# Decoder of two layers on one Trainium2 core: TensorE's order pinned by a fixed table in the stage of the heads of 16 and layer 0's experts

## The chip, the cores and the metric

One core of one Trainium2 chip runs the whole decoder in one launch. The metric is the device time of one execution in microseconds (us); several executions are compared by their median. The core has five engines that work at the same time, each through a queue of its own: TensorE (PE in the profile, with PEld for its loads of the stationary operand), VectorE (DVE), ScalarE (ACT), GpSimd (POOL) and SyncE (SP, which here issues DMAs). They meet at semaphores: an instruction waits until the results that it needs, or the buffer that it writes, are free.

## The reference

Everything is in 32-bit floats; the batch has 8 rows of 256 tokens of width 256. Cut to what matters here:

```python
x = x + L0_attn(layernorm(x))          # 16 heads of 16, rotary, biases
x = x + L0_xattn(ctx, layernorm(x))    # 16 heads of 16, keys and values are ctx itself, masked by length
x = x + L0_ffn(layernorm(x))           # experts that choose tokens, below
x = x + L1_attn(layernorm(x))          # 16 heads of 16, rotary, causal
x = x + L1_xattn(layernorm(x), ctx)    # 16 heads of 64, one null key and value
x = x + L1_ffn(layernorm(x))           # 8 experts, top 1, and a shared one

def L0_ffn(x):
    t = log(clip(x @ gate_w, 1e-6))                    # [b, n, 8]
    for _ in range(8):                                 # Sinkhorn
        t = t - logsumexp(t, axis=tokens)
        t = t - logsumexp(t, axis=experts)
    vals, idx = top_k(exp(t) per expert, n // 8)       # each expert takes 32 tokens of a row
    out = (x[idx] @ experts[e]) * vals
    return zeros.at[idx].set(out)                      # the last writer of a token wins
```

The case is about the first four lines (and of the fifth only the tables that are made for it).

## The kernel before, in words

x stays in SBUF as 16 tiles of 128 tokens by 256; tiles 2b and 2b+1 are row b of the batch. The first stage is a list of 24 *units*, each the attention of one row. Units 0 to 15 are layer 0's, in groups of four: self-attention of rows b and b+1, then cross-attention of the same two. Units 16 to 23 are layer 1's causal self-attentions. Beside them run the experts of layer 0, `chosen_experts`, for two rows at a time, as soon as the cross-attentions of those rows are done; layer 1's unit of a row needs the experts of the row.

A unit's **core** (`attention`, line 309) has four steps (c, kt): half c of the heads, half kt of the keys. A step is `scores` (eight matmuls of heads of 16, packed 32 rows a piece, into one tile `st`, line 326), two exponentials on ScalarE of 128x1024 each (`pT`, line 337; in layer 1 GpSimd then clears what is not causal, line 340), and `values` (sixteen matmuls into `o`, line 362, where the padded values carry a column of ones that yields the denominator). After kt = 1, `divided_T` (lines 395 to 405) on VectorE turns `o` by query, divides, and turns it back: `by_q`, `dens`, `att`, `attT`.

Ahead of a self-attention's core, `prepare` makes the layernorm (`norm_stats`, lines 252 to 257: statistics and small sums on VectorE, the power on GpSimd, then `normed`, line 261), transposes it (`tr`, line 284, copied by ScalarE), projects queries and keys (`qk`) and values (`v`) through `product` (line 275) for each half t of the tokens, turns them by rotary (lines 410 to 426), adds them up (`qkr`, line 462, on GpSimd for t = 0 and VectorE for t = 1), transposes keys and queries (`kT`, `qps`, line 471), and makes the masked queries `qm` (lines 305 on VectorE and 306 on ScalarE). Behind the core, `end` projects the output (`ao`) and adds it to x (line 489). A cross-attention needs only the transposed norm (`qpsx`, line 540) ahead, and `oR` (line 554) behind.

The experts: for each of two rows a norm (`xnb`), its transpose, the gate's product `lg` and `g` (line 641); then eight times a column sum by TensorE (`cs`) and a chain of six instructions on VectorE (lines 650 to 657); then `vps` (line 663), the top tokens of each expert (lines 669 to 673, a chain of twenty-one instructions on VectorE), which go through DRAM (`slots`, lines 676 to 682) and come back as rows and columns (`idx_row`, `by_half`, `cps` at line 687); then for each row `pick` (line 699, GpSimd), the rows taken by TensorE (`rps`, `rT`), the experts' products `y`, and the products that put them back (`back`, added at line 755).

[...] `mm`, three buffers of one bank, for all products and transposes; `scp`, one buffer of four banks, for `st`; `op`, one buffer of one bank, for `o`. So scores wait until the exponentials of the step before have read `st`, and values of a new half wait until `by_q` has read `o`.

**The order before.** `core()`, `prepare()`, `end()` and `chosen_experts()` are generators. The loop over units (below) advances the core and hands out pieces of the neighbours (`beside`) and of the experts at each yield; this is the program's order. From it a planner makes every engine's queue by its own estimate of when operands are ready, and by priorities: the last three quarters of the scores are drawn forward by `tc.high_priority(offset=AHEAD)`, with `AHEAD = 400` instructions. So the planner may put scores, or one of the other products, between the matmuls of a group of values. Six empty yields stand between the DMAs of the slots and `cps`. `tables_x` (norms, `wn`, `nvs`, `nvw` of the next stage) comes before the last unit's core, `weights_x` when all experts are done.

## Time and profile before

| what | value |
|---|---|
| time before, median of 3 runs | 1284.95 us (1284.14 to 1289.21) |
| the profiled execution, its own time | 1284.25 us |
| its span in the trace | 1282.4 us |
| first stage, first scores to the last of its products | 25.5 to 541 us |
| median of a scores matmul (128x512), of a values matmul | 587 ns, 379 ns |
| exponential of 128x1024, with and without the bias of the keys | 1110 ns, 1019 ns |
| `by_q` transpose on VectorE | 716 ns |
| power of a norm on GpSimd | 699 ns |

The profile is of one execution. Its page gives each engine's busy time and share of the span, then the span in 40 slices, each digit the busy share in tenths; PEclk is the TensorE clock that was granted, in tenths of full speed. Every group of instructions is named by line, engine, operation and the tiles that it writes and reads. "idle before" is time in which an engine stood still ahead of a group, with the instruction that released it. A timeline row has start, duration, engine, line, and the number of instructions; matmuls of 32-bit floats appear twice in these counts. Matmuls are pipelined, so the distance from start to start of two groups tells more than a duration. A row of stretches has the stretch, its length, then busy time and number of instructions of PE, PEld, DVE, ACT and POOL, the mean granted clock, the DMA share and GB/s.

### The profile page before, as it was taken

To read this page: it belongs to the slowest core of one execution; us is meant where nothing else is said; L and a number is where in the kernel's file an instruction comes from. 1 tells how busy PE (TensorE), PEld (TensorE's weight loads), DVE (VectorE), ACT (ScalarE), POOL (GpSimd) and SP (SyncE) were. 2 spreads that over 40 slices of the span, in tenths; PEclk is the share of its full clock that TensorE was granted. 3 is DMA by queue.
4 is the path that set the end of the run, shared out by engine and by line. 5 is a ranking of instruction groups with operands and counts; after the bars stand their busy time and mean duration, and the time that the engine had idled before them with its cause. 6 is when DMAs were issued, how large, how long until landed. Compare 5 with 4: busy or idle time off the path is not lost.

```text
span 1282.4 us, 28726 instructions
## 1 busy us (share of the span) xinstructions
PE 1200.1 (94%) x12188; PEld 726.8 (57%) x12188; DVE 585.2 (46%) x1632; ACT 438.6 (34%) x672; POOL 372.0 (29%) x450
## 2 busy tenths in 40 slices
PE   6889899799898989799999999999999999999997
PEld 2324344344344444457666666667676466888874
DVE  5455665755675765532333233324232657222213
ACT  2445445444434434213223232323142332122220
POOL 4322132141143454203242332414142514200004
PEclk8999899799899999999999999999999999999999
DMA  9990000000000041001010101020211205499934
GB/s 300 341 296 18 9 26 9 18 18 1 9 1 2 10 149 75 1 17 35 18 35 18 35 18 35 18 51 2 51 29 33 76 1 214 181 409 403 407 132 135
DMA packets 46923, 116.59 MB, mean 91 GB/s; under 512 B 8272, under 2 KB 30400, under 8 KB 42432
## 3 DMA queue, kind: packets, MB, share of 16 engines
q1 hardware_dynamic: 38912, 92.74, 21.2%
q0 software_dynamic: 5152, 18.89, 4.0%
q10 hardware_dynamic: 2720, 3.02, 0.7%
q8 instruction: 98, 1.61, 0.5%
q14 instruction: 41, 0.34, 0.1%
HBM read 104.00 MB, written 27.93 MB: 103 GB/s over the span
## 4 chain that ended last, share of the span: by engine, by line
PE 74%; DVE 9%; POOL 2%; issue 2%; ACT 1%; DMA 1%; SPq 0%; POOLq 0%; ACTq 0%; DVEq 0%
PE h L275 7%; PE v L275 7%; PE k L275 6%; PE o L362 5%; PE wo L275 5%; PE ox L1387 4%; PE stx L1348 4%; PE out L1765 3%; PE out L1582 3%; PE h L970 3%; PE st L326 3%; PE q L275 3%; PE qk L275 2%; PE tr L284 2%; PE fm L275 2%
## 5 line engine op out<-in xcount | busy, mean ns | idle before, releaser
L337 ACT ACTIVATE pT<-st 128x1024 f32<-128x1024 f32 (+1 forms) x128 | 110.6, 915 | 103.2 <-PE st L326 93.1
L362 PE MATMUL o<-pT,padv 128*32 128x256 f32 (+1 forms) x1536 | 127.0, 384 | 11.7 <-DVE by_q L395 4.0
L1354 POOL TENSOR_TENSOR both<-pTx 128x512 f32<-128x512 f32 x64 | 82.1, 1308 | 44.6 <-ACT pTx L1352 38.9
L362 PEld LDWEIGHTS o<-pT,padv 128*32 128x32 f32 x1536 | 49.7, 112 | 75.6 <-issue 46.8
L275 PE MATMUL h<-xrT,w 128*64 128x128 f32 (+1 forms) x1936 | 87.0, 250 | 1.3 <-issue 1.3
L337 ACT ACTIVATE pT<-st,kbias 128x1024 f32<-128x1024 f32 x64 | 67.8, 1110 | 57.5 <-PE st L326 57.4
L275 PEld LDWEIGHTS h<-xrT,w 128*64 128x64 f32 x1936 | 84.5, 137 | 4.0 <-issue 1.8
L1352 ACT ACTIVATE pTx<-stx 128x1024 f32<-128x1024 f32 x64 | 62.3, 1021 | 41.5 <-PE stx L1348 26.2
L963 DVE TENSOR_TENSOR midr<-sl,h 128x128 f32<-128x128 f32 x102 | 29.4, 288 | 101.7 <-PE h L275 68.4
L275 PE MATMUL qk<-l_wqkv,xnT 128*64 128x512 f32 x256 | 72.0, 630 | 1.8 <-DVE col L689 1.1
L326 PE MATMUL st<-qm,kT 32*128 32x512 f32 (+1 forms) x512 | 67.1, 594 | 3.0 <-ACT qm L306 1.5
L962 ACT ACTIVATE sl<-h 128x128 f32<-128x128 f32 (+1 forms) x114 | 35.3, 310 | 95.6 <-PE h L275 56.6
L1348 PE MATMUL stx<-qTx,kTx 64*128 64x256 f32 x512 | 64.3, 391 | 2.5 <-ACT pTx L1352 2.5
L340 POOL TENSOR_SCALAR_AFFINE_SELECT pT<-pT 128x512 f32<-128x512 f32 x64 | 41.7, 662 | 79.6 <-ACT pT L337 79.6
L1387 PE MATMUL ox<-pTx,vx 128*64 128x256 f32 x512 | 62.3, 385 | 0.0
L257 POOL TENSOR_TENSOR lnrs<-lnve,mhalf 128x2 f32<-128x2 f32 x48 | 33.8, 708 | 97.0 <-DVE lnve L255 76.1
L275 PE MATMUL wo<-wout_x,oT 128*64 128x256 f32 x512 | 58.0, 379 | 0.0
L1348 PEld LDWEIGHTS stx<-qTx,kTx 64*128 64x128 f32 x512 | 46.1, 186 | 20.3 <-ACT pTx L1352 7.6
L395 DVE STREAM_TRANSPOSE by_q<-o 128x512 f32<-128x512 f32 x48 | 34.2, 713 | 48.6 <-PE o L362 48.3
L1442 POOL TENSOR_TENSOR oT<-oT,rs 128x512 f32<-128x512 f32 x30 | 37.3, 1274 | 65.6 <-DMA rs<-rd 65.6
L257 POOL TENSOR_TENSOR lxrs<-lxve,mhalf 128x2 f32<-128x2 f32 x8 | 5.6, 702 | 155.4 <-DVE sc L1101 123.9
L1387 PEld LDWEIGHTS ox<-pTx,vx 128*64 128x64 f32 x512 | 33.9, 136 | 26.4 <-issue 12.1
(366 smaller groups left out, 2182.6 us busy)
## 6 DMA issues: line engine op xcount, KB each, us to landing
w<-packs SPq DMA_DIRECT2D x22, 1408.0 KB
w<-packs SPq DMA_DIRECT2D x22, 768.0 KB
rs<-rd SPq DMA_DIRECT2D x16, 512.0 KB
packs<-L_ffn_w_eDF SPq DMA_DIRECT2D x8, 704.0 KB
packs<-L_ffn_w_eDF SPq DMA_DIRECT2D x8, 640.0 KB
packs<-L_ffn_w_eFD SPq DMA_DIRECT2D x8, 640.0 KB
ctxT<-ctx_T SPq DMA_DIRECT2D x8, 512.0 KB
wkv_x<-L_xattn_Wkv POOLq DMA_DIRECT2D x1, 4096.0 KB, 15.6
```

The lines of the kernel that those rows point to most:

```text
L257: nc.gpsimd.tensor_tensor(rs[:, :n], ve[:, :n], mhalf[:, :n], ALU.pow)
L275: nc.tensor.matmul(out[h], lhsT[:, h], rhs, start=start, stop=stop, skip_group_check=True)
L326: nc.tensor.matmul(st[:, r, :, :n], kT[rows, c, bass.ts(kt, P)], qm[rows, c, :, q0:], start=True, stop=True,)
L337: nc.scalar.activation(pT[:, :, :, :n], st[:, 2 * k : 2 * k + 2, :, :n], AF.Exp, scale=scale, **kb)
L340: nc.gpsimd.affine_select(out=pT[:, :, :, :P], in_=pT[:, :, :, :P], compare_op=ALU.is_ge, fill=0.0, base=0, pattern=[[0, 2], [0, 2], [1, P ...
L362: made = nc.tensor.matmul(o[HP * j : HP * j + HP, m, q0:], v_pad[:, kt, 8 * c + 2 * j + m, :], pTs[j // 2][:, j % 2, m, : S - q0], start=k ...
L970: nc.tensor.matmul(h, shared["ws13"][:, c, lo : lo + P], shared["xnT"][:, c, bass.ts(q, 2 * S)], start=c == 0, stop=c == 1)
L1348: nc.tensor.matmul(st[:, g, kt, :], kT[rows, c, bass.ts(kt, P)], qT[rows, c, :], start=True, stop=True)
L1352: nc.scalar.activation(pT, st, AF.Exp, scale=scale)
L1354: nc.gpsimd.tensor_tensor(both, pT[:, :, 0, :], pT[:, :, 1, :], ALU.add)
L1387: nc.tensor.matmul(o[XD * g : XD * (g + 1), i, :], v[:, kt, 2 * (c2 + i) + g, :], pT[:, g, kt, :], start=kt == 0, stop=kt == 1, skip_group ...
L1582: nc.tensor.matmul(ps, mid[:, i, lo : lo + P], w2[:, i, :], start=i == 0, stop=i == NFC - 1)
```

## The change

The arithmetic is the same, and so is the number of matmuls. What changes is who decides TensorE's order. The generators `core`, `prepare` and `end` become methods: a class `Core` with `scores(step)` and `values(step)`, and on the attentions `norm`, `rows`, `heads(t)`, `vals(t)`, `begin` and `out`. The program runs within `tc.manual_schedule(engines={PE})`, so that TensorE's queue is in program order, while the planner still orders the other engines' queues. For every step (n, k) of unit n the program is: the scores of the next step (at k = 3 those of the next unit's first step), the values of this step, then everything that a fixed table `sides[n, k]` holds. The table is filled once: norm of unit n at (n-2, 2), rows at (n-2, 3), heads at (n-1, 0), values at (n-1, 1), `begin` (kT, qps, qm) at (n-1, 2), output at (n+1, 0), in layer 1 at (n+1, 2) and (n+1, 3), and pieces of the experts by counts. `AHEAD` goes; instead `SOON = 60` raises the priority of norms, of `divided_T` and of the chain behind each column sum. In the experts the norm of the first row becomes a piece of its own, the norm of the second stands behind the first one's `lg`, the six empty yields become one, and `pick` is made one row ahead. `tables_x` moves behind the last unit's steps (after the last values, before the last output), `weights_x` to the end of unit 20, `slot_tables` to (3, 3), and `add_up` to (0, 1).

By lines, after: product 276, transposes 285, scores 328, exponentials 339, values 365, `divided_T` 390 to 400, `qkr` 460, output add 485, `qpsx` 539, `oR` 549, `g` 640, the chain 652 to 659, the top chain 671 to 675, `cps` 688, `pick` 699.

```diff
-AHEAD = 400
+SOON = 60
...
-    def attention(kT, qm, v_pad, scale, causal, bias, dens):
+    class Core:
+        def scores(self, step):
...
             for r in range(4):
-                with tc.high_priority(offset=AHEAD if r else 0):
-                    nc.tensor.matmul(
+                nc.tensor.matmul(
...
-        ahead = scores(0)
-        yield
-        for step in range(4):
-            now = ahead
-            if step % 2 == 0:
-                o, begun = op.tile([P, 2, S], F32, tag="o", name="o"), {}
-            if step + 1 < 4:
-                ahead = scores(step + 1)
-                yield
-            values(step, now, o, begun)
-            if step % 2:
-                divided_T(attT[:, step // 2, :], o, dens[:, step // 2, :])
-            yield attT
+        def values(self, step):
+            c, kt, q0 = self.queries(step)
+            if kt == 0:
+                self.o, self.begun = op.tile([P, 2, S], F32, tag="o", name="o"), {}
...
+            if kt:
+                with tc.high_priority(offset=SOON):
+                    divided_T(self.attT[:, c, :], o, self.dens[:, c, :])
...
+        def norm(self):
+            with tc.high_priority(offset=SOON):
+                self.xn = work.tile([P, 2, D], F32, tag="xn", name="xn")
+                mv, rs = norm_stats([x[:, 2 * self.b + t, :] for t in range(2)], 1e-5, small, "ln")
+                for t in range(2):
+                    self.head = normed(self.xn[:, t, :], x[:, 2 * self.b + t, :], mv, rs, t)
+
+        def rows(self):
+            self.xnT = transposed(self.xn, work, mm, "xnT")
+            self.qkr = work.tile([P, 2, 2 * D], F32, tag="qkr", name="qkr")
...
+        def normed_rows(b):
+            with tc.high_priority(offset=SOON):
+                mv, rs = norm_stats([x[:, 2 * (b0 + b) + t, :] for t in range(2)], 1e-5, small, "ln")
+                for t in range(2):
+                    normed(xn[:, 2 * b + t, :], x[:, 2 * (b0 + b) + t, :], mv, rs, t)
+
+        normed_rows(0)
+        yield
         for b in range(nb):
-            mv, rs = norm_stats([x[:, 2 * (b0 + b) + t, :] for t in range(2)], 1e-5, small, "ln")
-            for t in range(2):
-                normed(xn[:, 2 * b + t, :], x[:, 2 * (b0 + b) + t, :], mv, rs, t)
             xnT = transposed(xn[:, 2 * b : 2 * b + 2, :], work, mm, "xnT")
             yield
...
+            if b + 1 < nb:
+                normed_rows(b + 1)
             yield
...
-        for _ in range(6):
-            yield
+        yield
         cps = mm.tile([P, 2, 2 * nb], F32, tag="mm", name="cps")
...
-        for b in range(nb):
+        def picked(b):
             pick = bwork.tile([P, 2, S], F32, tag="pick", name="pick")
-            put = bwork.tile([P, 2, S], F32, tag="put", name="put")
             for t in range(2):
                 nc.gpsimd.tensor_scalar(pick[:, t, :], idx_row[:, b, :], tokid[:, t : t + 1], None, ALU.is_equal)
-            yield
+            picks.append(pick)
+
+        picked(0)
+        yield
+        for b in range(nb):
...
+    for n, u in enumerate(units):
+        if u.__class__ is SelfAttention:
+            beside(n - 2, 2, u.norm)
+            beside(n - 1, 0, partial(u.heads, 0), partial(u.heads, 1))
+            beside(n - 1, 1, partial(u.vals, 0), partial(u.vals, 1))
+            beside(n - 1, 2, u.begin)
+            beside(n - 2, 3, u.rows)
+            if u.layer:
+                beside(n + 1, 2, partial(u.out, 0)) if n + 1 < len(units) else None
+                beside(n + 1, 3, partial(u.out, 1)) if n + 1 < len(units) else None
+            else:
+                beside(n + 1, 0, partial(u.out, 0), partial(u.out, 1))
+    for n, u in enumerate(units):
+        if u.__class__ is CrossAttention:
+            beside(n - 1, 0, u.norm)
+            beside(n - 1, 1, u.vals)
+            beside(n - 1, 2, u.begin)
+            beside(n + 1, 0 if n == 15 else 2, u.out)
+    beside(0, 1, add_up)
+    beside(3, 3, slot_tables)
+    for i in range(3):
+        n = 4 * i + 5
+        experts_at(i, n, 2, 2, 1, 1)
+        experts_at(i, n + 1, *((1, 2, 2, 2) if i == 2 else (1, 1, 1, 1)))
+        experts_at(i, n + 2, *((0, 1, 0, 0) if i == 2 else (0, 1, 1, 1)))
+        if i < 2:
+            experts_at(i, n + 3, 1, 0, 0, 1)
+            experts_at(i, n + 4, 0, 1, 1, 1)
+            experts_at(i, n + 5, 0, 1, 1, 1)
+        else:
+            experts_at(i, n + 3, 1, 1, 1, 1)
+            experts_at(i, n + 4, 0, 1, 1, 1)
+    experts_at(3, 16, 1, 1, 1, 1)
+    experts_at(3, 17, 1, 2, 2, 2)
+    experts_at(3, 18, 1, 1, 1, 0)
+    experts_at(3, 19, 0, 1, 1, 2)
+    experts_at(3, 20, 1, 2, 0, 0)
...
+    order.enter_context(tc.manual_schedule(engines={mybir.EngineType.PE}))
...
     for n, u in enumerate(units):
...
+        for k in range(4):
+            if k < 3:
+                u.core.scores(k + 1)
+            elif n + 1 < len(units):
+                units[n + 1].core.scores(0)
+            u.core.values(k)
+            for made in sides[n, k]:
+                made()
...
+    wn, nvw, hot8 = tables_x(wd, wq_x, wout_x, nkrow, nvcol)
+    order.close()
+    for t in range(2):
+        units[-1].out(t)
```

## The prediction

> **What bounds the kernel now.** I read the page first, then the busy time by stage, then TensorE's waits in the first stage, then its timeline. On the page TensorE is the busy engine:

> ```profile
> PE 1200.1 (94%) x12188; PEld 726.8 (57%) x12188; DVE 585.2 (46%) x1632; ACT 438.6 (34%) x672; POOL 372.0 (29%) x450
> PEclk8999899799899999999999999999999999999999
> ```

> The 9s of PEclk give way to 8s and a 7 in the first third: there TensorE partly runs at half clock. The orders of all five engines behind the stage of the heads of 16 (from the context's first product on, 541 us) are the same in both kernels, so only 25 to 541 us counts:

> ```profile
> 25.00:123.00 98.00, 86.43 (x664) 32.91 (x668) 46.02 (x116) 48.84 (x58) 26.02 (x34) 0.94 0.72 240
> 123.00:213.00 90.00, 81.87 (x764) 37.35 (x759) 56.56 (x179) 41.20 (x49) 24.15 (x28) 0.92 0.06 16
> 213.00:303.00 90.00, 81.51 (x764) 37.31 (x756) 56.57 (x179) 41.31 (x49) 24.15 (x28) 0.92 0.06 16
> 303.00:368.00 65.00, 57.29 (x546) 26.04 (x542) 42.10 (x150) 30.59 (x35) 11.99 (x15) 0.92 0.02 5
> 368.00:541.00 173.00, 152.36 (x1528) 76.71 (x1524) 107.95 (x306) 69.31 (x105) 71.35 (x99) 0.99 0.12 44
> ```

> PE (third figure) is busy for 82 of 90 us; DVE (the next but one) has 33 us free in each such stretch. So DVE isn't the bound by its sum, only by the order in which it does things. TensorE's waits in this stage, about 54 us in all, lie behind DVE results (total, times, longest):

> ```profile
> PE cs L275 <- DVE g L657: 15.6, 13, 2.9
> PE tr L284 <- DVE qkr L462: 7.6, 9, 2.7
> PE oR L554 <- DVE attT L405: 7.5, 8, 1.5
> PE o L362 <- DVE by_q L395: 4.0, 3, 2.8
> ```

> The longest, then what follows it, and a group of values cut in two:

> ```profile
> 149.92 0.62 PE L275 MATMUL cs<-g,ones 128*64 128x16 f32 x8 [2.92 <-DVE g L657]
> ...
> 152.00:156.00 4.00, 3.54 (x30) 1.15 (x26) 2.55 (x9) 2.81 (x3) 1.61 (x2) 0.50 0.00 0
> 156.00:160.00 4.00, 3.08 (x18) 0.80 (x12) 2.43 (x9) 0.36 (x1) 0.00 (x0) 0.50 0.00 0
> ...
> 143.20 0.62 PE L362 MATMUL o<-pT,padv 128*32 128x256 f32 x2
> 143.75 1.14 PE L326 MATMUL st<-qm,memk 32*128 32x512 f32 x8
> ```

> After 2.92 us idle the granted clock (the third figure from the end) is 0.50 until about 163. The two rows of o take 0.55 us to the next start, though a sixteenth of a whole group (1.0 us, start to start) would be 0.06 each.

> [...] here 2.76 us (at 75) was enough, and 2.75 (at 476) wasn't, and the way back took up to 14 us. [...]

> **The change, part by part.** No matmul is added or removed. TensorE's order becomes next scores, values, side products, and the side products wait in that order.

> (1) TensorE's work in the stage, from start-to-start times of uncut groups: scores, 80 x 1.07 + 16 x 0.65 = 96; values, 80 x 1.0 + 16 x 0.57 = 89; fifteen self-attentions' qk (2 x 1.83), v (2 x 0.96), three groups of transposes (0.5 each) and ao (1.9), 9.0 each, 135, and 2 of unit 0; eight cross attentions at 1.3, 10; four expert pairs at 16.7 (two tr 1.0, two lg 1.14, eight cs 2.8, vps and cps 0.8, two of rps, y and back 11.0), 67; tables 6. Sum 405. Before took 515.5 (25.5 to 541): 405, 54 idle, about 23 of clock (54 us ran at half rate, by slices of 4 us, of which some 23 are loss), and 33 left, of which the cut groups (120 pieces of o rather than 96, 34 groups cut, 0.5 each) are 17. I take the whole 33 as gone. So 110 us are to be had, and the question is what waits come.

> (2) Gate of the exponentials. One st buffer: two exponentials of 1.02 and the latencies make it 3.27 us from scores to scores (3.45 in cross). A step with 1.07 + 1.0 of its own and under 1.2 of side products waits: 12 us in units 0 to 4 (about 1.0 a step), 6 in units 5 to 12. Where the masked queries follow transposes in the same slot the next scores can start 1.70 us after the transposes (513.73/514.26 to 515.96), with 1.0 of values over it only if these stand behind; in layer 1 four such starts and steps give 11. Sum 29.

> (3) Group starts: the experts' transposes (tr of xnb) stand right behind ao in units 5, 9 and 13. On DVE six statistics (0.4 each), six aggregations (0.12 to 0.18), two ao adds (0.42) and three small adds come first, then three powers one after another on POOL (L257, 0.70 each, of which the first two count), then xnx, then xnb: 4.3 + 1.0 + 1.6 + 1.1 = 8.0 us from ao's start; ao itself is 1.95. 6.0 us of stall, three times: 18. Scores, values and everything else queue behind it. In before the same transpose at 305.11 had no wait.

> (4) by_q (L390 after) behind LN on DVE, with one o buffer: the next values wait. In unit 6 DVE's queue has 26 instructions between ao's add and by_q: adds 0.8, six statistics 2.4, six aggregations 0.8, one chain of the column sums 0.9, small adds 0.4, four norms 1.5, 6.9 in all, and 1.6 of waiting for two powers; from 1.0 after ao's start by_q comes 9.5 to 10 later, where the values of step 2 are due 5.8 after it: 4.3. The same count gives unit 2 2.8, unit 10 2.5, and unit 14 7.0 (two column sums and LN together). Sum 17.

> (5) The top chain (DVE, 5.4 us in before, 159.45 to 164.85) stands ahead of by_q and of qm in units 8 and 12: o waits 1.7, scores for qm 2.3, cps for the slots' DMA 1.4, 5.4 each; the same in unit 15 4.5, in units 18 and 19 3.2. Sum 18.5. In before six idle steps lay over the slots (vps to pick 11.4 us, 158.4 to 169.8); now two steps of some 5 us do, which is where the 1.4 comes from. Pick stands one batch further ahead on POOL, before the powers and the causal masks: 0 to 1 us, taken at 0.

> (6) Two cs in one slot wait for DVE's chain of six (1.5 us with its latencies, up to 1.9): units 14 and 17, 3.6 + 7.3 = 11.

> (7) The end: nvw now stands after the last values, with byk and its sums on DVE before it; no attention lies beside it. 5 us (before: 1.6).

> (8) On SP's and POOL's queues: the slot tables three steps later, the weights of the next stage (4096 KB on POOL's queue, 15.6 us to landing) behind step (20,3), three units of some 17 us before their use: nothing. add_up in (0,1) lies beside scores; its ps no longer waits 2.0 for bvw ahead of the first units, and I let the first scores start at 24.5 rather than 25.5.

> Waits 29 + 18 + 17 + 18.5 + 11 + 5 = 98.5. Clock: stalls of over 2.75 us at three group starts cost 7 each as at 149.92 (14 us at half rate), with 6 for the others: 27. Stage end: 24.5 + 405 + 98.5 + 27 = 555, against 541: +14. The profiled run's own time is 1284.25 (span 1282.4 and 1.85 about it), 0.7 below the median; 1284.25 + 14 = **1298**.

> Bounds of what no row of before shows. Group starts: 3 us each if DVE's adds and statistics run closer than I walk them, 7 with every semaphore late: 9 to 21. Clock: 10 [...] to 60 (eight stalls at 7). The 33 left over: half may belong to the switches between products and stay: 0 to +16.

> **Rivals.** (A) Not slower: DVE keeps up. DVE has 33 us of slack in 90, and with LN, sums and divisions raised in priority, its chains may begin as soon as data is there. Items 3 to 6 are 64.5 us; at half, 32 go, and the clock falls to 12 (no stall over 2.75): 24.5 + 405 + 66 + 12 = 507.5, or 1284.25 − 33.5 = 1251. It decides as soon as waits and clock together stay under 111.5 (I have 125.5). For it: the whole pipeline has 110 us to win. Against: before's own 4.0 us of o behind by_q, at one buffer, shows DVE's queue already being late.
> (B) The pinned order is worth the planner's: waits 88, clock 23, 541 as before: 1284.
> (C) The clock compounds: eight stalls at 7 us rather than 27 in sum, 1298 + 29 = 1327. For: 54 us ran cold in before with hardly any idle over 2.7. [...]
> That the order isn't what the change says is out: TensorE's queue holds 96 whole groups of values in place of 120 pieces.

> **How the numbers follow.** Likeliest 0.48 (own range 1287 to 1312); A 0.26 (1235 to 1278); B 0.12; C 0.14. About 0.5% (6.4 us) is what a measurement tells from no change. Faster takes A less its edge, 0.25; same B and a little of the two beside it, 0.14; slower 0.61. The range reaches into A and C: 1258 to 1324.

> **What would show it.** Right: tr waiting for xnb three times for about 6 us, o for by_q in units 6, 10 and 14, PEclk 5 or 6 after each, stretch 123 to 303 longer than 180 us. Wrong: no wait of tr on xnb above 3 us, or a st-to-st of about 3.3 through units 0 to 4 with a stage end below 530; then A.

## The result

The changed kernel takes 1294.03 us (median of 5 runs, 1291.79 to 1296.44), the kernel before 1285.04 beside it (1284.14 to 1289.21): a ratio of 1.0063, 95% interval 1.0041 to 1.0085. It is a little slower, by 9 us.

The page of the changed kernel, TensorE's busy row and its granted clock:

```profile
PE 1171.2 (91%) x12188; PEld 721.7 (56%) x12188; DVE 582.7 (45%) x1632; ACT 438.2 (34%) x672; POOL 374.4 (29%) x450
PEclk8999998998998999899999999999999999999999
```

TensorE is busy for 29 us less with the same instructions, and yet the span is 9.9 longer: the work got cheaper, the waits grew. The stretches of the changed kernel cover the same units as those shown of before (0 to 4, 5 to 8, 9 to 12, 13 to 15, 16 to the end of the stage; stretch, length, busy time of PE, PEld, DVE, ACT and POOL, granted clock):

```profile
25.00:114.50 89.50, 72.88 (x650) 29.58 (x650) 42.08 (x102) 48.48 (x57) 23.75 (x30) 0.94 0.79 262
114.50:192.60 78.10, 62.51 (x630) 28.79 (x630) 47.05 (x159) 40.13 (x47) 16.45 (x20) 0.93 0.05 15
192.60:275.80 83.20, 71.96 (x759) 34.66 (x759) 53.64 (x178) 41.30 (x49) 24.34 (x28) 0.96 0.06 17
275.80:351.00 75.20, 57.70 (x612) 28.46 (x612) 46.95 (x162) 30.93 (x36) 14.38 (x18) 0.92 0.02 5
351.00:548.40 197.40, 166.27 (x1609) 83.00 (x1609) 116.98 (x331) 69.61 (x106) 79.04 (x107) 0.93 0.11 40
```

Before, these were 98, 90, 90, 65 and 173 us. So the change wins 27 us up to unit 12, gives 10 back in units 13 to 15, and 24 more from unit 16 on. The stage ends at 548.4, where it ended at 541.4, 7.0 later. The other 2.9 us of the span lie behind the stage and aren't the change's: that part has the same orders in both, the two traces agree in it within 0.1 us for its first 578 us, and over all kernels of this document it takes 739.6 to 746.1 us.

TensorE's waits in the stage, changed kernel (total, times, longest):

```profile
PE st L328 <- ACT qm L307: 29.1, 19, 5.3
PE tr L285 <- DVE xnb L262: 14.6, 3, 4.9
PE st L328 <- ACT pT L339: 14.3, 17, 2.1
PE cs L276 <- DVE g L659: 11.6, 5, 4.5
PE o L365 <- DVE by_q L390: 7.3, 5, 1.9
PE o L365 <- POOL pT L344: 5.6, 4, 2.5
PE nvw L829 <- DVE nvs L825: 4.3, 1, 4.3
```

Two of the kernel before:

```profile
PE st L326 <- ACT qm L306: 1.5, 3, 0.7
PE st L326 <- ACT pT L337: 1.3, 2, 1.1
```

The largest growth is in the scores, which wait for the masked queries and for the exponentials: 43.4 us, where it was 2.8. The transposes of xnb follow with 14.6.

To compare kernels I split the stage, from its first scores to the next stage's first product, into three: TensorE's idle time (the waits' view, which also counts about 1 us ahead of the first scores), what the lowered clock cost (one minus the granted clock), and the rest, which is work at full clock with all switches between products. Beside it stands the number of unbroken groups in TensorE's queue: matmuls of one line and the same tiles that follow each other.

| kernel | stage end | idle | clock | rest | groups |
|---|---|---|---|---|---|
| before | 541.4 | 56.4 | 26.3 | 433.3 | 477 |
| changed | 548.4 | 92.8 | 34.1 | 396.1 | 386 |

With the order in whole groups the work is 37 us cheaper; 36 were paid in waits and 8 in clock. The clock term of one profile is one draw: worked out from span and mean granted clock, the loss over the whole program is 38.3 us on average over the five executions of the changed kernel, and the executions of the kernel before spread by 3.4 to 3.8 us (standard deviation).

### The profile page after: what moved, and what is told of

The parts are those of the page before. It is cut to its first block, busy times and chain, and to the rows that moved or that the text cites. A ratio compares the mean times of both kernels' runs of the same rounds, so it can differ in the third digit from the quotient of the medians.

```text
span 1292.3 us, 28714 instructions
## 1 busy us (share of the span) xinstructions
PE 1171.2 (91%) x12188; PEld 721.7 (56%) x12188; DVE 582.7 (45%) x1632; ACT 438.2 (34%) x672; POOL 374.4 (29%) x450
## 3 DMA queue, kind: packets, MB, share of 16 engines
q8 instruction: 98, 1.61, 0.5%
## 4 chain that ended last, share of the span: by engine, by line
PE 65%; DVE 5%; issue 3%; POOL 2%; ACT 2%; DMA 1%; SPq 0%; DVEq 0%; ACTq 0%; POOLq 0%
PE h L276 7%; PE v L276 6%; PE k L276 5%; PE ox L1423 4%; PE wo L276 4%; PE stx L1384 4%; PE out L1801 3%; PE h L1006 3%; PE out L1618 3%; PE st L328 3%; PE o L365 3%; PE q L276 2%; PE qk L276 2%; PE fm L276 2%; PE hx L1006 1%
## 5 line engine op out<-in xcount | busy, mean ns | idle before, releaser
L365 PE MATMUL o<-pT,padv 128*32 128x256 f32 (+1 forms) x1536 | 104.9, 388 | 12.9 <-DVE by_q L390 7.3
L328 PE MATMUL st<-qm,kT 32*128 32x512 f32 (+1 forms) x512 | 73.8, 647 | 32.2 <-ACT qm L307 23.0
L365 PEld LDWEIGHTS o<-pT,padv 128*32 128x32 f32 x1536 | 42.1, 114 | 101.7 <-issue 48.9
L276 PE MATMUL qk<-l_wqkv,xnT 128*64 128x512 f32 x256 | 62.1, 628 | 0.7 <-ACT xnT L288 0.7
L258 POOL TENSOR_TENSOR lnrs<-lnve,mhalf 128x2 f32<-128x2 f32 x48 | 36.5, 772 | 88.4 <-DVE lnve L256 67.6
L390 DVE STREAM_TRANSPOSE by_q<-o 128x512 f32<-128x512 f32 x48 | 34.1, 711 | 54.6 <-PE o L365 54.6
L328 PEld LDWEIGHTS st<-qm,kT 32*128 32x128 f32 x512 | 21.9, 200 | 52.0 <-ACT qm L307 26.6
```

The costliest lines, as they stand in the source:

```text
L258: nc.gpsimd.tensor_tensor(rs[:, :n], ve[:, :n], mhalf[:, :n], ALU.pow)
L276: nc.tensor.matmul(out[h], lhsT[:, h], rhs, start=start, stop=stop, skip_group_check=True)
L328: nc.tensor.matmul(st[:, r, :, :n], self.kT[rows, c, bass.ts(kt, P)], self.qm[rows, c, :, q0:], start=True, stop=True,)
L365: made = nc.tensor.matmul(o[HP * j : HP * j + HP, m, q0:], self.v_pad[:, kt, 8 * c + 2 * j + m, :], pTs[j // 2][:, j % 2, m, : S - q0], st ...
```

## The experiments

Each kernel starts from the changed one, if nothing else is said. Times are medians with the ratio to the kernel before and its 95% interval. The kernel before ran beside each, with medians of 1284.55 to 1287.93; the ratio isn't exactly the quotient of the two medians.

### The experts' norm one step earlier

```diff
-        experts_at(i, n, 2, 2, 1, 1)
+        beside(n - 1, 3, lambda i=i: next(ex[i], None))
+        experts_at(i, n, 1, 2, 1, 1)
```

> The first norm of the experts stands one step earlier, at (4,3), (8,3), (12,3). Theory 1 (a stall of TensorE behind VectorE's queue costs its idle time and the half clock after it): the three waits of tr for xnb, 14.6 us in all, fall below 1.5, the granted clock at these places stays at 0.9 or more (worth 8.5 us), and the stage's end moves from 548.4 to about 526. Rival (the norm's work only lands on another wait, by_q or qm): the end moves by less than 8.

1273.42 us, ratio 0.9911 (0.9883 to 0.9939): the stage ends at 528.3, 20.1 earlier. The three waits are now 1.0 us in all. Idle fell by 14.1, clock loss by 10.4 (to 23.7), the rest rose by 4.4. The changed kernel at unit 5, TensorE's timeline and VectorE's (start, duration, what ran, and in brackets the idle time before it):

```profile
119.78 1.95 PE L276 MATMUL ao<-l_wo,attT 128*64 128x256 f32 x16
126.50 1.12 PE L285 MATMUL tr<-ident,xnb 128*128 128x128 f32 x4 [4.78 <-DVE xnb L262]
127.55 1.24 PE L328 MATMUL st<-qm,kT 32*128 32x512 f32 x4
```

```profile
120.91 0.42 DVE L485 TENSOR_TENSOR x<-x,ao 128x256 f32<-128x256 f32 x1 [2.31 <-PE ao L276]
121.36 0.75 DVE L253 BATCH_NORM_STATS2 lnst<-x 128x6 f32<-128x256 f32 x2
...
124.39 0.31 DVE L256 TENSOR_SCALAR lnve<-lnmv 128x2 f32<-128x2 f32 x3
125.38 0.41 DVE L262 TENSOR_SCALAR xnx<-x,lnmv,lnrs 128x256 f32<-128x256 f32 x1 [0.68 <-POOL lnrs L258]
126.04 0.74 DVE L262 TENSOR_SCALAR xnb<-x,lnmv,lnrs 128x256 f32<-128x256 f32 x2 [0.24 <-POOL lnrs L258]
```

VectorE does three norms side by side, and the first xnb, which TensorE waits for, comes only after the statistics of all three. With the norm a step earlier the same place reads:

```profile
119.63 1.95 PE L276 MATMUL ao<-l_wo,attT 128*64 128x256 f32 x16
121.51 0.66 PE L285 MATMUL tr<-ident,xnb 128*128 128x128 f32 x4
122.10 1.14 PE L328 MATMUL st<-qm,kT 32*128 32x512 f32 x8
```

The scores start 5.45 us earlier, and at full clock: 1.14 us for eight rows, where above four took 1.24. The average clock loss of the executions fell as well, from 38.3 to 30.5. Theory 1 holds.

### The same stall, filled with work that nobody reads

```diff
+    def idle_work():
+        jk = mm.tile([P, 2 * D], F32, tag="mm", name="jk")
+        for _ in range(9):
+            nc.tensor.matmul(jk, ident, wqkv0[:, 0, : 2 * D], start=True, stop=True)
...
-        experts_at(i, n, 2, 2, 1, 1)
+        experts_at(i, n, 1, 0, 0, 0)
+        beside(n, 0, idle_work)
+        experts_at(i, n, 1, 2, 1, 1)
```

> Nine products of 128x512 that nobody reads (added work, some 4 us each time) stand between ao and tr of xnb in units 5, 9 and 13. The stall for xnb is then busy, not idle. If the clock falls because of these stalls: the clock loss goes from 34.1 to about 26, and the end moves by -5 to -9 with no wait of the program shortened. Rival (the clock is down for other reasons): loss above 31, the end moves by 0 to +3.

1293.12 us (1.0062, 1.0046 to 1.0078); the stage ends at 551.7. I had sized the filling wrongly: nine such products took 7.99 us, not 4, so the stalls of 4.9 were overfilled. The three terms still tell it: the rest rose by 27.5 (the filling), idle fell by 15.4 (the stalls), and the clock loss fell by 8.8, from 34.1 to 25.3; the sum is +3.3, as the end shows. Stretches of 4 us around the stall of unit 5, in the changed kernel, then with the filling:

```profile
121.00:125.00 4.00, 0.72 (x8) 0.20 (x4) 3.60 (x17) 0.00 (x0) 0.35 (x1) 0.90 0.01 2
125.00:129.00 4.00, 2.50 (x12) 1.20 (x12) 2.12 (x6) 0.58 (x1) 1.81 (x3) 0.50 0.00 0
129.00:133.00 4.00, 4.00 (x48) 1.87 (x44) 1.51 (x5) 2.40 (x3) 0.00 (x0) 0.74 0.00 0
```

```profile
125.00:129.00 4.00, 4.00 (x11) 1.84 (x10) 2.12 (x6) 0.00 (x0) 1.61 (x3) 1.00 0.00 0
129.00:133.00 4.00, 4.00 (x50) 2.05 (x47) 0.98 (x3) 2.51 (x3) 0.00 (x0) 1.00 0.00 0
```

The clock (third figure from the end) stays at 1.00. So each of these three stalls of 4.8 to 4.9 us cost about 2.9 us more afterwards (8.8 in all), through the clock alone. The executions agree: their average clock loss is 29.9 us (14 executions), 38.3 in the changed kernel.

### A cut in every group of values

```diff
-        def values(self, step):
+        def values(self, step, between):
...
-            if k < 3:
-                u.core.scores(k + 1)
-            elif n + 1 < len(units):
-                units[n + 1].core.scores(0)
-            u.core.values(k)
+            def between():
+                if k < 3:
+                    u.core.scores(k + 1)
+                elif n + 1 < len(units):
+                    units[n + 1].core.scores(0)
+            u.core.values(k, between)
...
                 for j in range(4):
+                    if (m, j) == (0, 1):
+                        between()
                     made = nc.tensor.matmul(
```

> Pinned as in the changed kernel, but the next step's scores stand between the first matmul of a group of values and the other seven, in nearly all of the 96 groups. Stage length is split into idle, clock loss and rest (396.1 in the changed kernel, 433.3 before). Theory (a cut costs about 0.5 us, and cuts are what the rest lost): rest rises by 40 to 50. Rival (the 37 lie in something else, such as the switches between small products): rest rises by less than 15.

1331.22 us (1.0346, 1.0318 to 1.0374). A step's scores are four matmuls and its values eight; the eight and sixteen named above are the profile's counts, which hold each twice. One cut in TensorE's timeline:

```profile
142.08 0.62 PE L367 MATMUL o<-pT,padv 128*32 128x256 f32 x2
142.63 1.14 PE L328 MATMUL st<-qm,kT 32*128 32x512 f32 x8
143.70 1.06 PE L367 MATMUL o<-pT,padv 128*32 128x256 f32 x14
```

The single matmul takes 0.55 us to the next start, an eighth of a whole group 0.13. The rest rose from 396.1 to 443.9: 47.8 us for 85 more groups, 0.56 each. The kernel before has 91 more groups than the changed one and a rest that is 37.2 longer, 0.41 each. So cuts are dear enough to be what the pin saves. But of the 91 only 24 are of values, and 51 are of the projections qk and v; what a cut of those costs by itself wasn't tried.

### The same program, order left to the planner

```diff
     units[0].norm()
...
-    order.enter_context(tc.manual_schedule(engines={mybir.EngineType.PE}))
     units[0].rows()
```

> The program of the changed kernel, with TensorE's order left to the planner. If the pin loses in the late units and gains in the early ones: groups of values are cut again, TensorE's waits fall below 60 us, and unit 13 starts later than with the pin (277) and the stage's end lies within 8 us of the kernel before's (541). Rival (the pin is a gain throughout and the table alone a loss): the end lies above 555.

1301.25 us (1.012, 1.0093 to 1.0146), end at 556.1: the first theory's 541 plus or minus 8 is missed, the rival's bound of 555 just passed. Idle is 60.3, clock 29.6, the rest 440.8 with 503 groups. Against the pinned kernel that is 44.7 more rest for 117 more groups (0.38 each) and 32.5 less idle. It isn't the planner's order of the kernel before: AHEAD is gone here too. From unit 13's first exponentials to the end it takes 268.1 us, the pinned one 271.3, the kernel before 238.0. So what is lost in the late units is not the pin: the rest of the change loses it with either order. That is the places of the side products, and also the priorities, pick made ahead and the later tables, which this run doesn't separate. In the early units (from the first exponentials to unit 13's) it is 259.7 against 249.6 pinned and 275.8 before: there the pin brings 10 us of its own.

### The last values of a unit before the next unit's first scores

```diff
-            elif n + 1 < len(units):
-                units[n + 1].core.scores(0)
             u.core.values(k)
+            if k == 3 and n + 1 < len(units):
+                units[n + 1].core.scores(0)
```

> At k = 3 the values of the step stand before the next unit's first scores. Theory 1: the waits of scores for qm, 29.1 us in 19 places, fall to 12 or less, the end of the stage moves by about -15. Rival (the exponentials and all behind them only come later): the waits for pT grow by as much, the end moves by 0 to -5.

1307.29 us (1.0168, 1.0138 to 1.0197), end at 561.8: 13 us slower, and here the rival was right and even too mild. The waits for qm fell from 29.1 to 14.2, those for the exponentials rose from 14.3 to 26.0, those for the causal masks from 5.6 to 9.0 and those for the slots from 0.8 to 3.5; idle is 95.5 in all. The timeline of the changed kernel at unit 1, then of this one:

```profile
47.74 1.14 PE L328 MATMUL st<-qm,kT 32*128 32x512 f32 x8 [1.56 <-ACT qm L307]
48.81 1.07 PE L365 MATMUL o<-pT,padv 128*32 128x256 f32 x16
51.00 1.14 PE L328 MATMUL st<-qm,kT 32*128 32x512 f32 x8 [1.12 <-ACT pT L339]
```

```profile
47.56 1.14 PE L328 MATMUL st<-qm,kT 32*128 32x512 f32 x8 [0.41 <-ACT qm L307]
50.81 1.14 PE L328 MATMUL st<-qm,kT 32*128 32x512 f32 x8 [2.12 <-ACT pT L339]
51.88 1.83 PE L365 MATMUL o<-pT,padv 128*32 128x256 f32 x16
```

The values that once lay under the exponentials were used up before them. Two groups of scores now follow each other with one st buffer between, and the idle time joins into one piece of 2.12 us; the values behind it run at a lower clock (1.83 us). Clock loss rose by 11.7, and that is most of the 13.

### A projection behind the queries' transposes

```diff
-            beside(n - 1, 1, partial(u.vals, 0), partial(u.vals, 1))
-            beside(n - 1, 2, u.begin)
+            beside(n - 1, 1, partial(u.vals, 0))
+            if n:
+                sides[n - 1, 2].insert(0, u.begin)
+            beside(n - 1, 2, partial(u.vals, 1))
```

> The second half's value projection v of a self-attention stands right behind the transposes that make its masked queries, and in layer 1 these stand ahead of the output product. Theory (0.96 us of TensorE's own work covers the wait for qm): scores waiting for qm fall from 29.1 to 18 or less, the waits for pT grow by no more than 4, the end moves from 548.4 to about 538. Rival (as with the values first: the wait only changes its name): the sum of the two waits, 43.4, stays within 4.

1289.84 us (1.0053, 1.0033 to 1.0073), which overlaps the changed kernel's interval; its profiled run ends the stage at 548.3, no earlier. The waits did go: for qm 29.1 to 15.0, for pT 14.3 to 16.3, idle down 8.2 in all. So the rival is out: the sum of the two, 43.4, is 31.3. But the rest rose by 4.6, the clock loss by 3.5 (about the spread of single executions), and values wait 3.3 more for by_q. Inconclusive as a gain: the cover is real, and it was given back in places that this run doesn't separate.

### The null value's column loaded early

```diff
-        nvcol = wd.tile([P, 1], F32, name="nvcol")
-        for g in range(2):
-            nc.sync.dma_start(nvcol[XD * g : XD * (g + 1), :], nkv[1:2, :].rearrange("o d -> d o"))
...
+    nvcol = const.tile([P, 1], F32, name="nvcol")
...
         if n == 2:
+            for g in range(2):
+                nc.sync.dma_start(nvcol[XD * g : XD * (g + 1), :], a["L1_xattn_null_kv"][1:2, :].rearrange("o d -> d o"))
```

> The null value's column is loaded with layer 1's weights in unit 2 rather than with the next stage's weights. Theory 1 (VectorE stands 2.8 us for that DMA, and qm of unit 21 with it): the wait of the scores at 483 falls from 5.3 to about 2.5, the end moves by -3 to -6 with the clock. Rival (the three norms ahead of qm are the cause): the wait stays at 4.5 or more, the end moves by less than 1.5.

1289.08 us (1.0024, 1.0008 to 1.004), end at 542.9, 5.5 earlier. VectorE's timeline in the changed kernel:

```profile
472.41 0.28 DVE L819 TENSOR_REDUCE own<-ident 128x2 f32<-128x128 f32 x1
474.23 0.69 DVE L755 TENSOR_TENSOR x<-x,back 128x512 f32<-128x512 f32 x1 [1.55 <-PE back L276]
477.70 0.16 DVE L820 TENSOR_TENSOR own<-own,nvcol 128x2 f32<-128x2 f32 x1 [2.78 <-DMA nvcol<-L_xattn_null_kv]
...
481.67 0.74 DVE L306 TENSOR_SCALAR qm<-qps,mask 128x512 f32<-128x512 f32 x1
```

A multiplication of 0.16 us for the next stage was put in VectorE's queue ahead of three norms and the masked queries; its operand was still on its way, and all behind it stood: the first norm reads the x that was added at 474.23, and began at 477.78. Unit 21's first scores came 5.3 us late. With the load early the norm begins at 475.47, right behind that add (474.75), and the scores wait 2.83 us. Theory 1 holds; in the 2.8 that stay VectorE's timeline shows the norms ahead of qm. The stage is 5.1 us shorter: 2.2 less idle time, 4.5 less clock, 1.6 more rest. The clock's part is partly luck of this execution: over 20 executions the loss is 36.8 on average, where it was 38.3. The medians, 1294.03 and 1289.08, put the whole at about 5 us.

### Doubled column sums at both ends of their slots

```diff
         for k, m in enumerate(counts):
-            beside(n, k, *[lambda: next(ex[i], None)] * m)
+            one_piece = lambda: next(ex[i], None)
+            if n in (14, 17) and m == 2:
+                sides[n, k].insert(0, one_piece)
+                m = 1
+            beside(n, k, *[one_piece] * m)
```

> In units 14 and 17 of the changed kernel a slot with two column sums has one of them at its front and one at its end, with the unit's own products between; nothing else is moved. Theory (two column sums in a row make TensorE wait for VectorE's chain): the waits of cs for g fall from 11.6 to 4 or less, units 14 and 17 (26.6 and 27.8) each get 2 to 5 shorter, the end moves from 548.4 to about 540. Rival (the chain is late behind norms and by_q anyway): cs still waits 8 or more, the end moves by less than 3.

1278.36 us (0.9959, 0.9944 to 0.9975), end at 536.3, 12.1 earlier. The waits of cs for g, 11.6 us before, are now:

```profile
PE cs L276 <- DVE g L659: 2.8, 1, 2.8
```

Unit 17 fell from 27.8 to 22.7 us, unit 14 from 26.6 to 24.3; the units behind them, 18 and 15, are 3.7 and 1.8 shorter as well, which the theory did not count. It holds in the waits and in the end.

### All of it

The early norm, the early column, the cover and the split sums together, with the next stage's tables two units earlier from buffers of their own:

```diff
-            byk = work.tile([P, XH, XD], F32, tag="pT", name="byk", bufs=4)
+            byk = tw.tile([P, XH, XD], F32, tag="byk", name="byk")
...
-        nvs = work.tile([P, nc8, P], F32, tag="pT", name="nvs", bufs=4)
+        nvs = tw.tile([P, nc8, P], F32, name="nvs")
...
+            if (n, k) == (22, 1):
+                tabled = tables_x(wd, wq_x, wout_x, nkrow, nvcol)
+                next(tabled)
+            if (n, k) == (23, 1):
+                wn, nvw, hot8 = next(tabled)
```

> The early norm, the null column early, v behind the queries' transposes, the doubled column sums of units 14 and 17 set at both ends of their slots, and the tables of the next stage two units earlier from buffers of their own. If the stalls add up: end at about 503 to 508, time about 1250. Rival (each gain lands on the next wait): 1262 or more.

1258.21 us (0.9787, 0.9754 to 0.9819), end at 515.2, between theory and rival. One new wait is in it, in unit 21, TensorE's timeline and VectorE's:

```profile
473.85 1.51 PE L365 MATMUL o<-pT,padv 128*32 128x256 f32 x12 [12.59 <-DVE by_q L390]
```

```profile
464.55 1.22 DVE L803 TENSOR_TENSOR byk<-wq_x,nkrow 128x1024 f32<-128x1024 f32 x1 [9.47 <-DMA wq_x<-L_xattn_Wq]
```

It is the null column's story again, with a larger load. So the last kernel loads the query weights ahead of the 4 MB, and raises the priority of masked queries and causal masks:

```diff
-        nc.gpsimd.dma_start(wkv_x, a["L1_xattn_Wkv"].rearrange("(c p) f -> p c f", p=P))
         nc.gpsimd.dma_start(wq_x, a["L1_xattn_Wq"].rearrange("(c p) f -> p c f", p=P))
         nc.gpsimd.dma_start(wout_x, a["L1_xattn_Wout"].rearrange("(c p) f -> p c f", p=P))
+        nc.gpsimd.dma_start(wkv_x, a["L1_xattn_Wkv"].rearrange("(c p) f -> p c f", p=P))
...
+            with tc.high_priority(offset=150):
+                qm = masked_queries(work, qps, mask2)
...
+                    with tc.high_priority(offset=150):
+                        nc.gpsimd.affine_select(
```

> As the combined kernel before, with the next stage's query weights loaded ahead of its 4 MB key and value weights, and a higher priority for the masked queries and the causal masks. Theory (VectorE stood 9.5 us for the query weights, and values waited 12.6 for by_q behind it): that wait goes, the end moves from 515 to 500 or less, the time from 1258 to about 1243. Rival (another of VectorE's queue waits takes the place): 1252 or more.

1248.49 us (0.9713, 0.968 to 0.9746), end at 508.9, again between theory and rival. It beats both kernels: 36 us under the one before, on the chip of that run. Idle 58.7, clock 23.0, rest 401.8: the pinned order's cheap work, with as little waiting as the planner had. The wait of 12.6 is 3.9 now; 7.2 us for the causal masks and 12.0 for qm remain (6.0 and 12.1 in the kernel before this one), so the two priorities moved little.

## Why the prediction came out as it did

Forecast 1298 (1258 to 1324), slower; measured 1294.03, slower. The main line holds, by the profile and by experiment: the pin makes TensorE's work cheaper, and it is taken back by waits that are no longer filled, behind VectorE's queue (three times 4.8 to 4.9 us for xnb) and for the exponentials' one buffer (14.3), and by the clock behind them. That VectorE's queue runs strictly in its order was an assumption of the forecast; what the runs show is single places, 2.78 us for nvcol and 9.47 for wq_x, in which what stood behind came later. The size is less good than the total: the stage was to grow by 14 us and grew by 7.0, and the median came nearer because 2.9 us of the profiled run's 9.9 lie in a part that the change doesn't touch.

**(1) Work.** 438 of work and switches before, 405 after, was forecast; it measures 433.3 and 396.1. Taking the whole 33 as gone was right, though I could place only 17 of it in cut values. Most of the groups that went are of other products, 67 of 91; that these are the remaining time is likely at 0.41 us a group, but no experiment cut them alone.

**(2) Gates**, 29: the waits for pT are 14.3; of the 29.1 for qm, 5.3 and 3.9 have other causes (below), which leaves 19.9. Together 34.

**(3) xnb**, three times 6.0: 4.8 to 4.9 each, 14.6. The transposes started 6.7 us after ao did, where I had walked 8.0: VectorE stood 0.68 and 0.24 us for the powers, where I had counted 1.6.

**(4) and (5) by_q and the top chain**, 35.5: this term was too large. All waits for by_q are 7.3: 1.1, 1.5 and 0.8 in units 2, 6 and 10, where I had 2.8, 4.3 and 2.5, and 1.9 each in units 8 and 12, where I had 1.7. The scores behind the top chain of unit 15 waited 3.9 (4.5 with all else in the forecast), and unit 14's 7.0 came as cs waiting 4.5. Unit 6 shows what the walk had wrong: by_q starts 6.3 us after ao's add, where I had 8.5, for VectorE stood 0.4 us for a power rather than 1.6, and its instructions took 5.9 rather than 6.9. That the xnb stall ahead had let VectorE catch up is not the reason: with that stall gone, in the kernel with the early norm, the five waits for by_q are 7.3 as before.

**(6) and (7) Doubled sums and the end**, 11 and 5: 11.6, in which the 4.5 of unit 14 are counted, and 4.3.

**At nothing: wrong in two places**, and both add to the late units. In (8), "three units of some 17 us before their use: nothing" looked at TensorE's use of the weights only; VectorE's use of a column of the same loads came at once, and cost about 5 us (shown by the early load). And in (5) pick ahead on POOL, "0 to 1 us, taken at 0": four picks took 3.66 us before unit 16's causal masks, and values waited 2.51 for these; all such waits are 5.6 against 3.2 before. That was not tried alone.

**Sum of waits and clock.** 98.5 was forecast, 92.8 measured; so the total is right partly by luck: (4) and (5), too large by some 20, made up for gates, loads and picks that were too small. Clock 27 forecast, 34.1 measured; 8.8 of it is shown to follow from the three xnb stalls, where the forecast had 21. Its 7 us for each came from one stall of the kernel before, with 13.7 us at half rate behind it; here the three were followed by 6.8, 6.8 and 3.4. The other 25 us, where the forecast had 6, lie at the stage's start (5) and behind eight other waits, of 1.6 to 5.3 us.

**Where in time.** Units 0 to 12 won 27 us and the others lost 34. The early stretch 123 to 303 was to be longer than 180 us; the same units take 161. That sign of the forecast failed: the waits of (4) and (5) that were placed there came to little. The sign "PEclk 5 or 6" couldn't be seen on the page, whose slices are 32 us long; in slices of 4 us the clock behind the stall of unit 5 is 0.50.

**The rivals.** The planner's worth (1284) and the compounding clock (1327) missed. That VectorE keeps up (1251) is wrong for this table. A better table with earlier loads comes to 1248.49; that the two numbers are close is chance, for no run shows VectorE keeping up by itself.

## What to carry to other kernels

When an engine's order is pinned, price two things apart: the whole groups (here 0.38 to 0.56 us for each group that goes) and the waits that can no longer be filled. For each pinned product, look in the other engines' queues for what stands ahead of its operand, small instructions for a later stage and their loads included (here 2.78 and 9.47 us). A wait removed by moving a filler can come back elsewhere, as with the values first, or gain nothing, as with the cover. What gained here was to begin the operand earlier, or to put work between two links of the same chain.

## What the runs showed of the hardware

Nearly equal idle time cost differently: with 92.8 us of it the clock took 34.1 us, with the 95.5 us of the kernel with the values first 45.8. The clock records of the twelve traces show why.

So in these traces half clock went with little work in a window, not with the length of a wait. This settles what the forecast had left open, 2.76 us of idle at 75 and 2.75 at 476 in the kernel before. The first lies in one window, the second is shared by two:

```profile
74.47:77.88 3.41, 0.65 (x8) 0.17 (x4) 2.70 (x8) 2.67 (x3) 2.10 (x3) 1.00 1.06 388
77.88:81.30 3.42, 3.42 (x22) 0.93 (x20) 0.78 (x2) 0.68 (x1) 0.00 (x0) 0.50 1.04 340
...
473.83:477.24 3.41, 1.94 (x20) 0.84 (x16) 3.34 (x13) 1.46 (x3) 1.44 (x3) 1.00 0.97 389
477.24:480.66 3.42, 1.89 (x14) 1.12 (x14) 1.94 (x4) 1.03 (x2) 0.87 (x2) 1.00 1.02 424
480.66:484.07 3.41, 3.12 (x44) 1.62 (x44) 0.47 (x1) 1.12 (x2) 0.00 (x0) 1.00 0.99 417
```

In the changed kernel a single wait of 1.60 us was enough: its window, from 404.12, had 1.81 us of work, and half clock followed for 3.4 us. A window at half clock loses 1.7 us, half of its 3.41, and the stalls of 4.8 to 4.9 for xnb cost two such windows, two and one. The kernel with the values first has 16 stretches at half clock from its first scores on, the changed one 11. So the same wait cost clock in one trace and none in another: values wait 1.9 us for by_q in units 8 and 12 of both the changed kernel and the one with the early norm; in the first it is the wait of unit 8 that is followed by half clock, in the second that of unit 12.
